# Starting each group's sums with a ScalarE copy into PSUM instead of identity matmuls, and splitting B in place

## The chip, the cores and the metric

The kernel runs on one core of a Trainium2 chip. Its engines work side by side, each through its own queue in order: TensorE (PE) multiplies matrices into the memory called PSUM, VectorE (DVE) does elementwise work and the scans, ScalarE (ACT) does activations and copies, GpSimd (POOL) does elementwise work on SBUF, and SyncE (SP) issues the transfers (DMA). The metric is the device time of one execution in microseconds. Of the kernel before there are three such times, 11,150.11, 11,154.43 and 11,172.63 us; the median is 11,154.43.

## The reference

A hybrid of four layers works on x of shape (4, 64, 64, 96): four images of 64x64 pixels with 96 channels. Layers 0 and 1 are state-space layers, layers 2 and 3 are attention without a softmax followed by a feed-forward network in rounded formats. Each of the first two is x + layer(group_norm(x)), and inside the layer stand an input projection to 192 channels and a gate, a 3x3 depthwise convolution with silu, and then the part that fills the time, a scan over the 4096 pixels in K = 4 orders:

```
x_dbl = einsum('bkdl,kcd->bkcl', xs, x_proj_w)       # xs: the image in the 4 orders
dts, Bs, Cs = split(x_dbl, [R, R + N], axis=2)       # R = 6, N = 16
delta = softplus(einsum('bkrl,kdr->bkdl', dts, dt_w) + dt_b)
def step(h, inp):
    h = exp(dt_t[..., None] * A) * h + (dt_t * u_t)[..., None] * B_t[:, :, None, :]
    y = einsum('bkdn,bkn->bkd', h, C_t)              # sum over the N = 16 states
out_y = ys + Ds.reshape(K, D)[None, :, :, None] * xs # the skip
y = y1 + y2 + y3 + y4                                # the 4 orders, put back in image order
```

In layer 0 the orders are rows, columns and both backwards; in layer 1 they are rows and windows of 2, 4 and 8 pixels. After it come a normalisation over the 192 channels, the gate, and the output projection.

## The kernel before

The scans of layers 0 and 1 run in four phases (`phases`): two layers times two pairs of images. Within a pair, 64 channels of each image fill the 128 partitions, so 192 channels are J = 3 slices j. A phase has 16 blocks (`blocks`): four orders k times four stretches t of TB = 1024 pixels. A block has 48 tiles: for g in 0, 1 (states 0 to 7, then 8 to 15), for j in 0, 1, 2, for the eight states n. That makes 64 blocks and 3072 tiles, and 384 groups of eight tiles.

Each tile works on 128x1024 numbers. ScalarE makes the decays exp(delta*A) (`decays`, line 669). For 11 of the 16 states TensorE spreads a row of B over the partitions into PSUM (`row`, line 662) and VectorE multiplies it by delta*u there (`product`, line 676); for the five states of POOL_N GpSimd multiplies instead (`begin`, line 652). VectorE scans (`scan`, line 684), ScalarE keeps the last state (line 690), GpSimd multiplies the states by C (`weigh`, line 695), and TensorE adds every two tiles into the group's PSUM tile `psY`, of which there is one, with eight matmuls (`gather`, line 727).

The sums of a group do not start from zero. `resume` (line 706) puts into psY what there is so far, by a matmul with the identity: for g = 1 the half sum `ysum` that ScalarE copied out of psY after g = 0 (`flush`, line 739); for g = 0 the sums `yold` of the earlier orders from DRAM, put in this order's pixel order by the operand's view (`resumed` in `pieces`); and for g = 0, k = 0 the convolved image, multiplied by the skip weights through a diagonal matrix `dg` that `skips` makes. After g = 1, `flush` copies the sums back in image order to `ynew` (line 743) and sends them to DRAM. Behind each group's last addition stand thus the flush on ScalarE, then the seed on TensorE, then the next group's first addition.

Once per block `prepare` makes the next block's inputs at fixed tiles: loads, the projection of xs to 76 rows (line 543, PSUM tile `pps`), delta (569 to 582), and a split of B and C into three bfloat16 parts (`parts`) that add up to the float32 value. Part q is cut by ScalarE (`cut`, line 559); `take` (lines 564 and 565) then makes a PSUM tile with the float32 value, by an identity matmul, less the parts so far, by matmuls with `minus`, from which the next part is cut.

The order of every compute engine's queue is written by hand, by a loop over i from -9 to the last tile plus 3. In turn i come begin(i+2), flush(i-3) where a group ends, gather(i-2) for odd tiles, row(i+2), scan(i), the late decays(i+2), product(i+1), weigh(i), the tasks of `prepare` due at this tile, one step of an aside generator (the next phase's convolution, the former phase's normalisation and projection) and last resume(i-2) where a group begins. There are six f tiles, two PSUM tiles `psB`, two `psM` and four `part` tiles (yold, ysum, ynew).

Of the kernel before, what the change touches and what calls it, by code (L numbers as in the profile page):

```python
# [8 lines left out]
F32 = mybir.dt.float32  # L9
# [3 lines left out]
AF = mybir.ActivationFunctionType  # L13
# [21 lines left out]
def kernel(ctx: ExitStack, tc: tile.TileContext, ins, out, layers=(0, 1, 2, 3)):  # L35
    nc = tc.nc
# [7 lines left out]
    def st(shape, dtype, tag, bufs, name=None):  # L44
        return sp.tile(shape, dtype, tag=tag, name=name or tag, bufs=bufs)
# [17 lines left out]
    def part(shape, name):  # L63
        return st(shape, F32, "part", 4, name)
# [44 lines left out]
    minus = wp.tile([96, 2 * N], BF16, tag="minus", name="minus")  # L109
# [25 lines left out]
    W = {}  # L135
# [13 lines left out]

    def skips(li):  # L150

        dsum = small([128, J, 1], "dsum")
        nc.vector.reduce_sum(dsum, W[li]["ds"], axis=mybir.AxisListType.X)
        dg = W[li]["dg"] = st([128, J, 128], F32, "dg", 1)
        for j in range(J):
            nc.scalar.activation(dg[:, j, :], ident, AF.Copy, scale=dsum[:, j, :])

    def tail_weights(li):

# [290 lines left out]
    def pieces(li, k, t):  # L450

        if li == 0:
            if k in (0, 2):
                tt = t if k == 0 else NTB - 1 - t
                img = lambda v: v[:, tt * TB : (tt + 1) * TB]
                view = lambda v: v if k == 0 else v[:, ::-1]
                return img, [(view, lambda o: o)], lambda py, v: [
                    (py[:, s * T : (s + 1) * T], view(v)[:, s * T : (s + 1) * T]) for s in range(2)  # L460
                ]
# [8 lines left out]
            return img, [(view, lambda o: o.rearrange("p (w h) -> p w h", h=HW))], lambda py, v: [  # L470
                (py[:, s * T : (s + 1) * T], view(v)[:, s * cols // 2 : (s + 1) * cols // 2]) for s in range(2)
            ]
        img = lambda v: v[:, t * TB : (t + 1) * TB]
        if k == 0:
            return img, [(lambda v: v, lambda o: o)], None
# [14 lines left out]

        def resumed(py, v):
            v = v.rearrange("p (a i b j) -> p a b i j", i=s, j=s, b=HW // s)
            return [(py[:, a * TB // n : (a + 1) * TB // n], v[:, a]) for a in range(n)]

        return img, [by_row(r) for r in range(s)] if s < n else [by_band(a) for a in range(n)], resumed

    def imaged(li, k, v):

# [2 lines left out]
    def prepare(ph, k, t):  # L501
# [2 lines left out]


        li = phases[ph][0]
        img, views, resumed = pieces(li, k, t)
        p = {"views": views, "img": img, "resumed": resumed, "dus": [None] * J, "deltas": [None] * J}
# [3 lines left out]
        taken = {}  # L512

        def weights():
            if li not in W:
                W[li] = scan_weights(li)
            if t == 0 and k == 0 and "dg" not in W[li]:
# [37 lines left out]
            nc.sync.dma_start(p["bc"][:, halves[s]], rests[s][0 : 4 * N])  # L555

        def cut(s, q):
            of = taken.pop(s) if q else pps[s][0 : 2 * N]
            nc.scalar.copy(p["parts"][32 * q : 32 * q + 32, halves[s]], of)

        def take(s, q):
            of = taken[s] = psM([2 * N, T])
            part = slice(0, 32 * q + 32)
            nc.tensor.matmul(of, ident[0 : 2 * N, 0 : 2 * N], rests[s][0 : 2 * N], start=True, stop=False)
            nc.tensor.matmul(of, minus[part], p["parts"][part, halves[s]], start=False, stop=True)

        def steps(s, j):
            pds.append(psM([128, T]))
# [128 lines left out]

    def recall(i):  # L700
        at, g, j, n = tiles[i]
        ph, k, t = blocks[at]
        sums[at, j] = imaged(phases[ph][0], k, part([128, TB], "yold"))
        nc.sync.dma_start(sums[at, j], made[at]["img"]((yd if k else xcd)[ph][:, j, :]))

    def resume(i):
        at, g, j, n = tiles[i]
        ph, k, t = blocks[at]
        py = sums[at, g, j] = psY()
        old = sums.pop((at, j))  # L710
        of = W[phases[ph][0]]["dg"][:, j, :] if g == 0 and k == 0 else ident
        if g == 0 and k:
            parts = made[at]["resumed"](py, old)
        else:
            parts = [(py[:, s * T : (s + 1) * T], old[:, s * T : (s + 1) * T]) for s in range(2)]
        banks = len(parts) * T // TB
        for m, (o, v) in enumerate(parts):
            nc.tensor.matmul(o, of, v, start=(m % banks == 0), stop=False)  # L718

    def gather(i):  # L720
        at, g, j, n = tiles[i]
        py = sums[at, g, j]
        two = [scanned.pop(e)[1] for e in (i - 1, i)]
        for s in range(2):
            ss = slice(s * T, (s + 1) * T)
            for e in range(2):
                nc.tensor.matmul(  # L727
                    py[64 * e : 64 * e + 64, ss], fold, two[e][:, ss],
                    start=False, stop=(n == g * GN + GN - 1),
                )  # L730

    def flush(i):

        at, g, j, n = tiles[i]
        ph, k, t = blocks[at]
        py = sums.pop((at, g, j))
        if g < NG - 1:
            sums[at, j] = part([128, TB], "ysum")
            nc.scalar.copy(sums[at, j], py)  # L739
            return  # L740
        yb = imaged(phases[ph][0], k, part([128, TB], "ynew"))
        for src, dst in made[at]["views"]:
            nc.scalar.copy(src(yb), dst(py))  # L743
        nc.sync.dma_start(made[at]["img"](yd[ph][:, j, :]), yb)
# [217 lines left out]
    phases = [(li, pair) for li in (0, 1) if li in layers for pair in range(pairs)]  # L962
# [34 lines left out]
    def behind(ph):  # L997
# [9 lines left out]
        if ph + 1 == len(phases):  # L1007
# [4 lines left out]
    tiles = [(at, g, j, n) for at in range(len(blocks)) for g in range(NG) for j in range(J)  # L1012
             for n in range(g * GN, (g + 1) * GN)]
    per = NG * J * GN
    made, reps, sums, states, scanned, order = {}, {}, {}, {}, {}, [None]
    end = len(tiles)
    now, rest = [0], (L - TB) // 256
    with tc.manual_schedule(engines=MANUAL):
        convs = [conv(0)]
        while done[0][0] < TB // T:  # L1020
            next(convs[0])
# [24 lines left out]
        for i in range(-9, end + 4):  # L1046
# [5 lines left out]
                begin(i + 2)  # L1052
            if 0 <= i - 3 < end and tiles[i - 3][3] % GN == GN - 1:
                flush(i - 3)
            if 0 <= i - 2 < end and tiles[i - 2][3] % 2:
                gather(i - 2)
            if 0 <= i + 2 < end:
# [9 lines left out]
            at, place = divmod(i, per)  # L1067
            now[0] = i
            if 0 <= i < end:
# [20 lines left out]
                if aside is not None and not (plan and place in kept):  # L1090
                    advance()
                    if holds == MORE and late_by(i, blocks[at][0]):
                        advance()
            if 0 <= i - 2 < end and tiles[i - 2][3] % GN == 0:
                resume(i - 2)
        now[0] = end + per

        def remaining():
# [113 lines left out]
```

## Time and profile before

| | |
|---|---|
| profiled execution, its own time | 11,149.85 us |
| its span | 11,148.1 us |
| median of three runs | 11,154.43 us |
| mean granted TensorE clock | 0.870 |
| busy PE / DVE / ACT / POOL | 8910.0 / 9926.4 / 6423.1 / 10204.6 us |
| transfers | 66.1% of the 16 DMA engines' time |
| the first scan starts at / the last one | 134.5 us / 10,543.3 us |

A group of instructions is told by its line, engine, operation, written and read tiles, and shapes with its count; then come its busy time in us and the mean of one in ns, then the idle time of its engine just before them and what ended it. In the list of waits the columns are who waited for whom, the sum in us, how many times, and the longest.

### The profile page before, as it was taken

To read this page: it belongs to the slowest core of one execution; us is meant where nothing else is said; L and a number is where in the kernel's file an instruction comes from. 1 tells how busy PE (TensorE), PEld (TensorE's weight loads), DVE (VectorE), ACT (ScalarE), POOL (GpSimd) and SP (SyncE) were. 2 spreads that over 40 slices of the span, in tenths; PEclk is the share of its full clock that TensorE was granted. 3 is DMA by queue.
4 is the path that set the end of the run, shared out by engine and by line. 5 is a ranking of instruction groups with operands and counts; after the bars stand their busy time and mean duration, and the time that the engine had idled before them with its cause. 6 is when DMAs were issued, how large, how long until landed. Compare 5 with 4: busy or idle time off the path is not lost. (4 is left out here: it accounts for less than half of the span.)

```text
span 11148.1 us, 101994 instructions
## 1 busy us (share of the span) xinstructions
PE 8910.0 (80%) x30112; PEld 2880.5 (26%) x30112; DVE 9926.4 (89%) x6431; ACT 6423.1 (58%) x10575; POOL 10204.6 (92%) x5102
## 2 busy tenths in 40 slices
PE   7978888777777779887788878887778877778777
PEld 2222222111222212221222222222222322222365
DVE  3898999999999889989999999999999999999846
ACT  3656556554566646665566656665466655555576
POOL 3989999999999889999999999999999999999846
PEclk8989999888888889998888889998888888888877
DMA  5679976897578885798666656665556565556410
GB/s 134 158 141 162 141 160 157 145 134 136 149 171 151 140 151 149 157 159 132 138 169 157 157 146 169 164 159 143 149 157 156 155 149 148 143 137 159 122 33 22
DMA packets 1848188, 1604.57 MB, mean 144 GB/s; under 512 B 1412298, under 2 KB 1482892, under 8 KB 1847628
## 3 DMA queue, kind: packets, MB, share of 16 engines
q1 hardware_dynamic: 1847628, 1598.04, 66.1%
q8 instruction: 237, 3.88, 0.2%
q14 instruction: 323, 2.65, 0.1%
HBM read 1008.37 MB, written 186.65 MB: 107 GB/s over the span
## 5 line engine op out<-in xcount | busy, mean ns | idle before, releaser
L695 POOL TENSOR_TENSOR f<-f,crep 128x1024 f32<-128x1024 f32 x3072 | 7158.9, 2354 | 395.9 <-DVE f L684 296.6
L727 PE MATMUL psY<-f,fold 128*64 128x512 f32 x12288 | 3795.1, 698 | 183.4 <-POOL f L695 182.8
L684 DVE TENSOR_TENSOR_SCAN f<-f,state,psB 128x1024 f32<-128x1024 f32 x1584 | 3717.8, 2347 | 206.2 <-ACT f L669 50.1
L669 ACT ACTIVATE f<-delta,L_a 128x1024 f32<-128x1024 f32 x2112 | 2406.5, 1145 | 903.9 <-PE psY L727 829.8
L676 DVE TENSOR_TENSOR psB<-psB,du 128x1024 f32<-128x1024 f32 x2112 | 2558.9, 1212 | 362.9 <-PE psB L662 322.1
L662 PE MATMUL psB<-spB,sel 96*128 96x512 bf16 x4224 | 1387.8, 414 | 1613.5 <-DVE f L684 1599.0
L652 POOL TENSOR_TENSOR f<-du,brep 128x1024 f32<-128x1024 f32 x960 | 2265.7, 2360 | 127.2 <-PE psY L727 29.4
L684 DVE TENSOR_TENSOR_SCAN f<-psB,state,f 128x1024 f32<-128x1024 f32 x720 | 1676.7, 2329 | 76.8 <-POOL f L652 50.3
L727 PEld LDWEIGHTS psY<-f,fold 128*64 128x64 f32 x12288 | 974.9, 154 | 2525.3 <-issue 1806.8
L690 ACT COPY state<-f 128x1 f32<-128x1 f32 x2304 | 429.7, 188 | 2065.8 <-DVE f L684 2056.7
L669 ACT ACTIVATE psB<-delta,L_a 128x1024 f32<-128x1024 f32 x960 | 1070.2, 1115 | 696.0 <-DVE f L684 636.1
L684 DVE TENSOR_TENSOR_SCAN f<-f,psB 128x1024 f32<-128x1024 f32 x528 | 1208.3, 2288 | 57.6 <-ACT f L669 5.9
L662 PEld LDWEIGHTS <-sel 96*128 96x128 bf16 x4224 | 271.3, 99 | 3320.4 <-DVE f L684 2163.7
L289 PE MATMUL psM<-pad,wf 96*64 96x512 f32 x3456 | 901.4, 623 | 36.0 <-ACT pad L283 28.9
L684 DVE TENSOR_TENSOR_SCAN f<-psB,f 128x1024 f32<-128x1024 f32 x240 | 545.6, 2273 | 102.9 <-ACT psB L669 60.0
L718 PE MATMUL psY<-ysum,ident 128*128 128x512 f32 x768 | 554.5, 862 | 98.3 <-ACT ynew L743 86.7
L585 POOL TENSOR_TENSOR xs<-delta,xs 128x1024 f32<-128x1024 f32 x192 | 452.7, 2358 | 95.0 <-ACT delta L582 95.0
L569 PE MATMUL psM<-proj,dtw 12*128 12x512 f32 x768 | 455.2, 686 | 0.0
L543 PE MATMUL psM<-xs,xp 128*76 128x512 f32 x768 | 414.7, 651 | 5.5 <-DMA xs<-xcd 4.2
L718 PE MATMUL psY<-yold,ident 128*128 128x512 f32 (+2 forms) x960 | 370.6, 526 | 42.2 <-ACT ysum L739 26.7
L289 PEld LDWEIGHTS psM<-pad,wf 96*64 96x64 f32 x3456 | 221.4, 138 | 501.0 <-issue 422.6
L743 ACT COPY ynew<-psY 128x1024 f32<-128x1024 f32 (+2 forms) x312 | 242.4, 818 | 171.5 <-PE psY L727 171.5
(149 smaller groups left out, 6644.6 us busy)
## 6 DMA issues: line engine op xcount, KB each, us to landing
crep<-bc SPq DMA_DIRECT2D x2048, 256.0 KB, 4.8
delta<-delta SPq DMA_DIRECT2D x768, 256.0 KB, 4.8
du<-xs SPq DMA_DIRECT2D x768, 256.0 KB, 6.2
brep<-bc SPq DMA_DIRECT2D x640, 256.0 KB, 4.9
yd<-ynew SPq DMA_DIRECT2D x192, 512.0 KB, 7.8
xraw<-xcd SPq DMA_DIRECT2D x144, 512.0 KB, 8.5
yold<-yd SPq DMA_DIRECT2D x144, 512.0 KB, 8.9
xcd<-xo SPq DMA_DIRECT2D x96, 256.0 KB, 3.0
```

The source lines that it names most:

```text
L289: nc.tensor.matmul(px[64 * i : 64 * i + 64], w["wf"][:, tap, 64 * j : 64 * j + 64], pads[i][0][:, tap // 3 : tap // 3 + rows, tap % 3 : ta ...
L569: nc.tensor.matmul(pds[-1], order[0][1][64:76, j, :], rests[s][64:76], start=True, stop=True)
L585: nc.gpsimd.tensor_mul(xs[j], deltas[j], xs[j])
L652: nc.gpsimd.tensor_mul(f[:, 1:], made[at]["dus"][j][n % 2], reps[at, 0, n])
L662: nc.tensor.matmul(scanned[i][0][:, ss], sel[:, n, :], made[at]["parts"][:, ss], start=True, stop=True)
L669: nc.scalar.activation(out, made[at]["deltas"][j][n % 2], AF.Exp, scale=W[phases[ph][0]]["a"][:, k, j, n // 2 : n // 2 + 1])
L676: nc.vector.tensor_mul(scanned[i][0], scanned[i][0], made[at]["dus"][j][n % 2])
L684: nc.vector.tensor_tensor_scan(f[:, 1:], a, bu, 0.0 if t == 0 else states[at - 1][:, c : c + 1], ALU.mult, ALU.add)
L690: nc.scalar.copy(states[at][:, c : c + 1], f[:, TB : TB + 1])
L695: nc.gpsimd.tensor_mul(f[:, 0:TB], f[:, 1:], reps[at, 1, n])
L718: nc.tensor.matmul(o, of, v, start=(m % banks == 0), stop=False)
L727: nc.tensor.matmul(py[64 * e : 64 * e + 64, ss], fold, two[e][:, ss], start=False, stop=(n == g * GN + GN - 1),)
```

## The change

The seed of a group's sums moves from TensorE to ScalarE: `resume` now copies the sums so far into psY with ScalarE, scaled by the skip weight itself where k = 0, in the views of `pieces` for the other orders. `dg` and `resumed` go. Since no matmul starts psY's accumulation any more, `unlock` writes all of psY with matmuls once at the very start, and `gather` adds to what is there. In the loop `resume(i-2)` moves from the end of the turn to just behind the flush of the group before. Beside it, `take` no longer makes a PSUM tile of its own: it subtracts each part from the projection's own PSUM tile, where `cut` reads the next one.

```diff
     def skips(li):
-        dsum = small([128, J, 1], "dsum")
+        dsum = W[li]["skip"] = small([128, J, 1], "dsum")
         nc.vector.reduce_sum(dsum, W[li]["ds"], axis=mybir.AxisListType.X)
-        dg = W[li]["dg"] = st([128, J, 128], F32, "dg", 1)
-        for j in range(J):
-            nc.scalar.activation(dg[:, j, :], ident, AF.Copy, scale=dsum[:, j, :])
...
         def cut(s, q):
-            of = taken.pop(s) if q else pps[s][0 : 2 * N]
-            nc.scalar.copy(p["parts"][32 * q : 32 * q + 32, halves[s]], of)
+            nc.scalar.copy(p["parts"][32 * q : 32 * q + 32, halves[s]], pps[s][0 : 2 * N])
 
         def take(s, q):
-            of = taken[s] = psM([2 * N, T])
-            part = slice(0, 32 * q + 32)
-            nc.tensor.matmul(of, ident[0 : 2 * N, 0 : 2 * N], rests[s][0 : 2 * N], start=True, stop=False)
-            nc.tensor.matmul(of, minus[part], p["parts"][part, halves[s]], start=False, stop=True)
+            part = slice(32 * q, 32 * q + 32)
+            nc.tensor.matmul(
+                pps[s][0 : 2 * N], minus[part], p["parts"][part, halves[s]], start=False, stop=True,
+                skip_group_check=True,
+            )
...
+    def unlock():
+        py = psY()
+        for s in range(2):
+            for q in range(T // 128):
+                o = s * T + q * 128
+                nc.tensor.matmul(py[:, o : o + 128], ident, ident, start=(q == 0), stop=True, skip_group_check=True)
+
...
         py = sums[at, g, j] = psY()
         old = sums.pop((at, j))
-        of = W[phases[ph][0]]["dg"][:, j, :] if g == 0 and k == 0 else ident
-        if g == 0 and k:
-            parts = made[at]["resumed"](py, old)
+        if g:
+            nc.scalar.copy(py, old)
+        elif k == 0:
+            nc.scalar.activation(py, old, AF.Copy, scale=W[phases[ph][0]]["skip"][:, j, :])
         else:
-            parts = [(py[:, s * T : (s + 1) * T], old[:, s * T : (s + 1) * T]) for s in range(2)]
-        banks = len(parts) * T // TB
-        for m, (o, v) in enumerate(parts):
-            nc.tensor.matmul(o, of, v, start=(m % banks == 0), stop=False)
+            for src, dst in made[at]["views"]:
+                nc.scalar.copy(dst(py), src(old))
...
                     py[64 * e : 64 * e + 64, ss], fold, two[e][:, ss],
-                    start=False, stop=(n == g * GN + GN - 1),
+                    start=False, stop=(n == g * GN + GN - 1), skip_group_check=True,
...
     with tc.manual_schedule(engines=MANUAL):
+        unlock()
         convs = [conv(0)]
...
                 flush(i - 3)
+            if 0 <= i - 3 < end and tiles[i - 3][3] % GN == GN - 1 and i - 2 < end or i == 2:
+                resume(i - 2)
             if 0 <= i - 2 < end and tiles[i - 2][3] % 2:
                 gather(i - 2)
...
-            if 0 <= i - 2 < end and tiles[i - 2][3] % GN == 0:
-                resume(i - 2)
```

More of the change, by code (lines that the diff above doesn't have):

```diff
@@ L458, in pieces @@
                 view = lambda v: v if k == 0 else v[:, ::-1]
-                return img, [(view, lambda o: o)], lambda py, v: [
-                    (py[:, s * T : (s + 1) * T], view(v)[:, s * T : (s + 1) * T]) for s in range(2)
-                ]
+                return img, [(view, lambda o: o)]
             cols = TB // HW
@@ L468, in view @@
                 return v if k == 1 else v[:, ::-1, ::-1]
-            return img, [(view, lambda o: o.rearrange("p (w h) -> p w h", h=HW))], lambda py, v: [
-                (py[:, s * T : (s + 1) * T], view(v)[:, s * cols // 2 : (s + 1) * cols // 2]) for s in range(2)
-            ]
+            return img, [(view, lambda o: o.rearrange("p (w h) -> p w h", h=HW))]
         img = lambda v: v[:, t * TB : (t + 1) * TB]
         if k == 0:
-            return img, [(lambda v: v, lambda o: o)], None
+            return img, [(lambda v: v, lambda o: o)]
         s = 1 << k
@@ L489, in by_band @@
             )
[L491 to L495, printed above, removed]
+        return img, [by_row(r) for r in range(s)] if s < n else [by_band(a) for a in range(n)]
     def imaged(li, k, v):
@@ L506, in prepare @@
         li = phases[ph][0]
-        img, views, resumed = pieces(li, k, t)
-        p = {"views": views, "img": img, "resumed": resumed, "dus": [None] * J, "deltas": [None] * J}
+        img, views = pieces(li, k, t)
+        p = {"views": views, "img": img, "dus": [None] * J, "deltas": [None] * J}
         xs, deltas = [], []
@@ L511, in prepare @@
         raws, pps, rests, pds = [], [], [], []
-        taken = {}
         def weights():
@@ L516, in weights @@
                 W[li] = scan_weights(li)
-            if t == 0 and k == 0 and "dg" not in W[li]:
+            if t == 0 and k == 0 and "skip" not in W[li]:
                 skips(li)
```

## The prediction, made before the result was known

> **What bounds the kernel now.** I read the page's busy times first, then engines by stretch, then the list of waits, then the groups by form of the lines that the diff touches, and last the timeline around one place where a group of eight states ends.
>
> ```profile
> PE 8910.0 (80%) x30112; PEld 2880.5 (26%) x30112; DVE 9926.4 (89%) x6431; ACT 6423.1 (58%) x10575; POOL 10204.6 (92%) x5102
> ...
> 135.00:351.00 216.00, 184.13 (x672) 53.51 (x672) 146.86 (x94) 104.41 (x153) 152.38 (x66) 0.92 0.55 139
> 1522.00:1676.00 154.00, 132.87 (x438) 35.53 (x438) 146.69 (x87) 95.25 (x140) 152.81 (x67) 0.93 0.74 170
> 5430.00:5599.00 169.00, 125.63 (x392) 39.53 (x392) 148.46 (x87) 96.85 (x185) 155.43 (x71) 0.87 0.65 154
> 9439.00:9901.00 462.00, 343.99 (x990) 97.99 (x990) 445.78 (x244) 240.57 (x373) 458.00 (x199) 0.85 0.59 146
> ```
>
> The columns of a stretch are its length, then busy PE, PEld, DVE, ACT, POOL, then granted clock. 154 us is one block (48 tiles) that runs well: POOL is busy for 152.8 of it. Three such blocks in a row (9439 to 9901) have POOL busy for 458 of 462. So a block has a floor of about 154 us, set by POOL, and nothing that PE or ACT saves can be seen there. What can be won lies in blocks above the floor: the first one (216 us, PE busy 184 beside the convolution) and those beside the normalisation and output projection (169 us and the like). Between 700 and 10400 us POOL is idle for 457 us (9700 less 9243 busy), in the first two blocks for 83 more (216+173 less 152.4+153.3). These 540 us are all that can be had from the scan.
>
> ```profile
> ACT f L669 <- PE psY L727: 829.8, 479, 6.0
> DVE psB L676 <- PE psB L662: 322.1, 242, 13.6
> POOL f L695 <- DVE f L684: 296.6, 212, 26.1
> DVE f L684 <- ACT psB L669: 84.2, 26, 26.1
> DVE f L684 <- ACT f L669: 57.9, 31, 8.0
> ```
>
> VectorE waits for TensorE's spread of B (L662) for 322 us, and GpSimd for VectorE's scan for 297. VectorE waits for ScalarE for only 142.
>
> ```profile
> 5006.51 3.68 PE L718 MATMUL psY<-yold,ident 128*128 128x512 f32 x4
> ...
> 5010.12 1.94 PE L727 MATMUL psY<-f,fold 128*64 128x512 f32 x8
> ...
> 5011.99 0.61 PE L662 MATMUL psB<-spB,sel 96*128 96x512 bf16 x2
> ...
> 5012.17 1.15 ACT L669 ACTIVATE f<-delta,L_a 128x1024 f32<-128x1024 f32 x1 [2.20 <-PE psY L727]
> ...
> 5012.63 1.23 DVE L676 TENSOR_TENSOR psB<-psB,du 128x1024 f32<-128x1024 f32 x1 [1.25 <-PE psB L662]
> ```
>
> Here the seed of the sums (L718), the first pair's addition (L727) and the next spread of B (L662) follow each other on PE without a gap; then ACT has waited 2.20 us for an f buffer and VectorE 1.25 us for its product. Numbering the scans in time and giving each wait of L676 to the scan after it, tile 5 of the eight (the first spread behind the seed in PE's queue) takes 111 us of VectorE's wait for PE and tile 6 takes 58: 169 us in 132 waits, the rest spread over six other places.
>
> **The change part by part.**
>
> ```profile
> L718 PE MATMUL psY<-ysum,ident 128*128 128x512 f32 x768 | 554.5, 862 | 98.3 <-ACT ynew L743 86.7 <-ACT state L690 10.0 <-ACT ysum L739 1.7
> L564 PE MATMUL psM<-proj,ident 32*32 32x512 f32 x512 | 273.2, 614 | 0.0
> L739 ACT COPY ysum<-psY 128x1024 f32<-128x1024 f32 x192 | 193.1, 1006 | 135.5 <-PE psY L727 121.0 <-issue 12.3 <-DMA brep<-bc 1.2
> L669 ACT ACTIVATE psB<-delta,L_a 128x1024 f32<-128x1024 f32 x960 | 1070.2, 1115 | 696.0 <-DVE f L684 636.1 <-PE psY L727 38.2 <-issue 11.0
> L743 ACT COPY ynew<-psY 128x1024 f32<-128x1024 f32 x120 | 163.2, 1360 | 101.3 <-PE psY L727 101.3
> ```
>
> *Seed leaves PE.* The five forms of L718 are busy 554.5+273.0+103.3+49.7+47.9 = 1028 us, 2.68 us at each of 384 boundaries. In the trace the first addition begins right behind the last seed matmul at all of them, on average 3.6 us after ScalarE's flush has ended.
>
> *Seed arrives on ACT.* No row shows a plain copy from SBUF into PSUM. Nearest are the plain copy out of PSUM (1.006 us) and the exponential into PSUM (1.115). So: 192 copies for g=1 at 1.006 = 193; 48 scaled ones (k=0) at 1.115 = 54; layer 0: 24 reversed at 1.01 = 24 and 48 transposed at 1.9 (the L743 row is 72 at 1.0 and 48 of these: 163.2-72 = 91) = 91; layer 1 in pieces: 96 of 512 elements at 0.58 = 56 and 96 of 256 at 0.378 = 36. Together 454 us, 1.18 per boundary; ACT goes from 6423 to some 6880 us (62%). With 1.115 for the plain ones it would be 475.
>
> *Where it stands in ACT's queue.* The seed now follows the flush at once; behind it are the state copy, decays into psB, and work of the asides. In 265 of 384 flushes the next ACT instruction follows within 0.3 us, so it is pushed by all 1.18. I pushed each by its seed's time, let ACT's later idle time absorb it, and set it against the time that each decay stands ready before its scan (median 2.2 us at the tightest places): VectorE would be late in 39 boundaries, 28 us in all. Taken: 28. Bounds: 0 (PE's earlier additions also end ACT's 830 us of waiting for f, so ACT may run earlier than before), and 1.18 at each of the 265, 313 us.
>
> *Seed to first addition.* The addition now waits for flush plus 1.18 us instead of 3.6: 2.4 us earlier, and so are the next spread of B and the release of f. If two thirds of the 169 us at tiles 5 and 6 go, VectorE is given 113 us. One third may stay because PE, arriving earlier, waits for ACT or GpSimd instead. Bounds: 0, and all 309 us of L676's waits in the scan.
>
> *What VectorE's time is worth.* From the third block on POOL is idle for 487 us and DVE for 715 (every gap over 0.03 us, initial two blocks left out): 0.68. So 113 gives 77, and the 28 cost 19. Bounds 0 and 1.
>
> *Split of B in place.* 512 ident matmuls (273 us) go; the 256 of L565 stay (64x32 and 32x32 weights take the same, 398 and 384 ns). They can run before the cut that L565 waits for, so they lie under ACT's work, save where PE is full. Same with the psM buffer that each took. The projection keeps both psM buffers until its last cut, in places where no aside runs; the steps behind it took them at the same places before. I count nothing but PE time; bounds -34 us (what ACT's L559 waits for L565 now) to +34.
>
> *First two blocks.* There PE is busy 184 of 216 and 158 of 173. It loses 16+4 us per block (1028 and 273 over 64). Half of it on the path: -20; bounds 0 and -40.
>
> *The rest.* Three 0.39 us scalings of ident per layer go: nothing. Eight unlocking matmuls of 0.3 us (the 128x128 form of L360) stand before the first convolution, whose inputs are then still being loaded: nothing, at most 2.4 us. No DMA is added or moved; yold has 31 us (nine tiles) from its issue to its use and lands in 8.5, so SP and POOL queues stay as they are.
>
> **A rule that speaks against it.** A less busy PE gets a lower clock in this trace: 0.93 at 86% busy (1522 to 1676) and 0.85 at 74% (9439 to 9901). PE at (8910-1301)/11150 = 68% would by that line fall from 0.87 to about 0.81, and 7609 us of matmuls become some 8170. PE keeps 740 us of its 1301, and I have the third that stays above for this. The Trainium skill (TensorE: Matmul & The Clock Gate, Part 1) has it that one idle window of about 3.4 us halves the clock. By that rule a boundary that goes idle would run its additions at half speed (1.94 us for eight becoming 3.37, as once at 5021 us); met at half of the boundaries, 1.43 of the 2.4 us would go there, and the 77 would be an estimated 54; by the rows it stays 77. The skill's PSUM page (summary of rules) advises against seeds that ScalarE writes, since its writes do not set the accumulate bits. No run here shows it, and the unlocking matmuls are there for that; either way no time changes.
>
> **Sum.** 11,149.9 (profiled execution; 0.04% under the median 11,154.4) -77 -20 +19 = 11,072 us. Against the 540 us that could be had this is a sixth.
>
> **The rivals.** *Much more is won:* earlier additions end most L676 waits and f waits. All 309 x 0.68 = 210, first blocks 40: 10,900. For it: the waits named; against: much of POOL's idle time is beside DMA and group statistics, which stay. *Nothing to be seen:* POOL hides it, 11,150 +-22. For it: the blocks at 154; against: those at 169. *Slower:* ScalarE's queue becomes what is late at each boundary. At its price, 313 x 0.68 = 213 against 97 won: 11,266. It decides from 0.37 us of VectorE's time per boundary on (97/0.68/384). For it: 265 flushes with ACT work close behind; against: median slack 2.2 us. *It does not do what it says:* with accumulate flags wrong the sums are wrong, the time the same.
>
> **How the numbers follow.** 0.2% (22 us) is about what a measurement of this kernel tells from no change. Likeliest case (11,000 to 11,128) 0.50; much more won 0.15; nothing 0.17; slower 0.18. The range takes half of each outer case: 10,960 to 11,190; the likeliest alone is 11,000 to 11,128. Faster 0.65, same 0.17, slower 0.18.
>
> **What would show it.** L718 gone from PE, PE near 8200 us, clock near 0.81, ACT near 6880; waits of L676 for L662 from 322 to about 200; waits of L684 for ACT from 142 to some 170; POOL's idle time 80 us less; blocks at 154 us unmoved, the first one some 10 us shorter. Wrong if waits for L669 pass 300 us, or if PE's first addition waits for ACT at most boundaries and L676's waits stay.

## The result and the profile after

The kernel with the change takes 11,231.25 us (median of four runs, 11,218.49 to 11,249.81) and the one before, run beside it, 11,163.53. The ratio is 1.0062 with an interval of 1.0039 to 1.0085: slower by 0.6%, where 11,072 us and a range up to 11,190 had been forecast. The profiled execution took 11,219.25 us (span 11,216.4) at a mean granted clock of 0.817.

The functions keep their names and get other lines: the scan is now L671, the product L663, the spread of B L649, the additions L722, the weighing L682, the decays L656, the matmuls to delta L556 with their ScalarE reader L563, the split's subtraction L549, and the seed L708 to L713. Below are the busy times of the page after:

```profile
PE 8392.2 (75%) x27696; PEld 2658.5 (24%) x27696; DVE 9925.7 (88%) x6431; ACT 6880.5 (61%) x11073; POOL 10199.9 (91%) x5102
```

VectorE and GpSimd do the work they did before (9926.4 and 10204.6 us), so the 68 us more are idle time of theirs. ScalarE has grown to the 6880 us that were forecast. TensorE lost 1301 us of matmuls and its busy time fell by only 518. The groups by form show where these stand (count, then busy us and mean ns of one, then idle time before them). Before, the additions and the matmuls to delta read:

```profile
L727 PE MATMUL psY<-f,fold 128*64 128x512 f32 x12288 | 3795.1, 698 | 183.4 <-POOL f L695 182.8
...
L569 PE MATMUL psM<-proj,dtw 12*128 12x512 f32 x768 | 455.2, 686 | 0.0
```

and after:

```profile
L722 PE MATMUL psY<-f,fold 128*64 128x512 f32 x12288 | 4271.3, 771 | 588.7 <-POOL f L682 264.9 <-issue 242.7 <-POOL f L639 43.2
...
L556 PE MATMUL psM<-proj,dtw 12*128 12x512 f32 x768 | 533.9, 793 | 0.2 <-ACT spB L545 0.2
...
L708 ACT COPY psY<-ysum 128x1024 f32<-128x1024 f32 x192 | 195.2, 1017 | 6.1
L713 ACT COPY psY<-yold 128x1024 f32<-128x1024 f32 x72 | 116.0, 1611 | 2.3
...
L710 ACT ACTIVATE psY<-yold,dsum 128x1024 f32<-128x1024 f32 x48 | 53.7, 1118 | 1.5
```

Together with two smaller forms of L713 (56.6 and 36.1 us) the seeds take 457.6 us of ScalarE; 454 had been worked out. The additions are the same 12,288 matmuls as before and take 771 ns each in place of 698; the matmuls to delta take 793 in place of 686. What stayed on TensorE thus grew from 7609 to 8392 us. Of the waits (who waited for whom, sum in us, times and longest) this is one before:

```profile
ACT delta L576 <- PE psM L569: 45.9, 57, 2.0
```

and after they read:

```profile
DVE psB L663 <- PE psB L649: 307.1, 220, 12.3
POOL f L682 <- DVE f L671: 301.9, 199, 27.7
...
ACT delta L563 <- PE psM L556: 143.2, 133, 2.8
DVE f L671 <- ACT psB L656: 140.2, 52, 27.8
...
DVE f L671 <- ACT f L656: 78.6, 38, 6.9
```

VectorE's wait for the spread of B, 322.1 us before, was to fall to about 200 and fell by 15. The wait for delta, 45.9 before, has trebled (143.2), though nothing was added in front of those matmuls. VectorE's waits for ScalarE rose from 142 to 219, still below the 300 that would have spoken for ScalarE's queue.

**Where the time goes, place by place.** I numbered the scans in time and took, for every place p in a block (counted from 0 to 47), the time between scan p and the next, after less before, summed over blocks 2 to 62; "tile 24" in such a sum is the step from scan 24 to scan 25, in which VectorE waits for tile 25's spread. The sum is +64.6 us. Tiles 4 and 5 of each eight, the boundary tiles, whose steps contain the waits behind the seed and the first addition in TensorE's queue, win 107.9 us. Everything else taken together loses 172.5: tiles 22 to 27 lose 51.4 (tile 24 alone 0.58 us per block, 35 in all), tiles 8 to 11 lose 40.8, 30 and 31 lose 23.4, 16 to 19 lose 19.8, 38 and 39 lose 18.4, the rest 18.7. In front of those blocks, the first scan starts at 128.4 in place of 134.5 us, block 0 takes 223.9 in place of 216.3 and block 1 171.2 in place of 173.3.

So the gain at the boundaries came, and more than that was lost elsewhere. This is TensorE's timeline around tile 24 of block 58, before (start, length, what it is, and in brackets the idle time ahead of it and what ended it):

```profile
9661.85 1.04 PE L564 MATMUL psM<-proj,ident 32*32 32x512 f32 x2
9662.82 0.39 PE L565 MATMUL psM<-spB,minus 64*32 64x512 bf16 x1
9664.39 0.60 PE L662 MATMUL psB<-spB,sel 96*128 96x512 bf16 x2 [1.19 <-DVE f L684]
9664.93 1.12 PE L569 MATMUL psM<-proj,dtw 12*128 12x512 f32 x2
9665.98 1.94 PE L727 MATMUL psY<-f,fold 128*64 128x512 f32 x8
9667.85 0.61 PE L662 MATMUL psB<-spB,sel 96*128 96x512 bf16 x2
```

and the same place after:

```profile
9714.30 0.39 PE L549 MATMUL psM<-spB,minus 32*32 32x512 bf16 x1
9718.51 0.82 PE L649 MATMUL psB<-spB,sel 96*128 96x512 bf16 x2 [3.83 <-DVE f L671]
9719.26 2.07 PE L556 MATMUL psM<-proj,dtw 12*128 12x512 f32 x2
9721.26 3.68 PE L722 MATMUL psY<-f,fold 128*64 128x512 f32 x8
9724.87 0.94 PE L649 MATMUL psB<-spB,sel 96*128 96x512 bf16 x2
```

and VectorE's next product after:

```profile
9725.85 1.23 DVE L663 TENSOR_TENSOR psB<-psB,du 128x1024 f32<-128x1024 f32 x1 [1.58 <-PE psB L649]
```

Without the identity matmuls of the split, TensorE idles 3.83 us here, where it had idled 1.19. The two matmuls to delta then take 2.07 us in place of 1.12, and the eight additions 3.68 in place of 1.94. The spread for the next tile, which comes behind them in TensorE's queue, is so late that VectorE stands still for 1.58 us. There are holes of more than 2.5 us ahead of tile 24's spread in none of the 61 blocks before and in 31 after; in all places, from the third block to the last scan, they grew from 221 to 337. Between the scans of tiles 24 and 26 the mean granted clock fell from 0.859 to 0.778.

### The profile page after: what moved, and what is told of

The parts are those of the page before. It is cut to its first block, busy times and chain, and to the rows that moved or that the text cites. A ratio compares the mean times of both kernels' runs of the same rounds, so it can differ in the third digit from the quotient of the medians.

```text
span 11216.4 us, 97704 instructions
## 1 busy us (share of the span) xinstructions
PE 8392.2 (75%) x27696; PEld 2658.5 (24%) x27696; DVE 9925.7 (88%) x6431; ACT 6880.5 (61%) x11073; POOL 10199.9 (91%) x5102
## 3 DMA queue, kind: packets, MB, share of 16 engines
q8 instruction: 218, 3.57, 0.1%
## 5 line engine op out<-in xcount | busy, mean ns | idle before, releaser
L682 POOL TENSOR_TENSOR f<-f,crep 128x1024 f32<-128x1024 f32 x3072 | 7156.5, 2354 | 428.7 <-DVE f L671 301.9
L722 PE MATMUL psY<-f,fold 128*64 128x512 f32 x12288 | 4271.3, 771 | 588.7 <-POOL f L682 264.9
L671 DVE TENSOR_TENSOR_SCAN f<-f,state,psB 128x1024 f32<-128x1024 f32 x1584 | 3717.7, 2347 | 216.2 <-ACT f L656 62.5
L649 PE MATMUL psB<-spB,sel 96*128 96x512 bf16 x4224 | 1478.2, 438 | 1912.4 <-DVE f L671 1877.6
L663 DVE TENSOR_TENSOR psB<-psB,du 128x1024 f32<-128x1024 f32 x2112 | 2557.7, 1211 | 345.1 <-PE psB L649 307.1
L656 ACT ACTIVATE f<-delta,L_a 128x1024 f32<-128x1024 f32 x2112 | 2405.7, 1144 | 660.5 <-PE psY L722 582.9
L722 PEld LDWEIGHTS psY<-f,fold 128*64 128x64 f32 x12288 | 1099.3, 167 | 3049.6 <-issue 2141.4
L671 DVE TENSOR_TENSOR_SCAN f<-psB,state,f 128x1024 f32<-128x1024 f32 x720 | 1677.5, 2330 | 121.8 <-ACT psB L656 60.9
L656 ACT ACTIVATE psB<-delta,L_a 128x1024 f32<-128x1024 f32 x960 | 1068.7, 1113 | 630.5 <-DVE f L671 588.7
L671 DVE TENSOR_TENSOR_SCAN f<-f,psB 128x1024 f32<-128x1024 f32 x528 | 1208.5, 2289 | 66.6 <-ACT f L656 13.0
L649 PEld LDWEIGHTS <-sel 96*128 96x128 bf16 x4224 | 282.8, 101 | 3773.9 <-DVE f L671 2513.8
L286 PE MATMUL psM<-pad,wf 96*64 96x512 f32 x3456 | 928.4, 639 | 60.9 <-ACT pad L280 45.7
L671 DVE TENSOR_TENSOR_SCAN f<-psB,f 128x1024 f32<-128x1024 f32 x240 | 545.4, 2273 | 118.7 <-ACT psB L656 76.1
L556 PE MATMUL psM<-proj,dtw 12*128 12x512 f32 x768 | 533.9, 793 | 0.2 <-ACT spB L545 0.2
L563 ACT ACTIVATE delta<-psM,L_dtb 128x512 f32<-128x512 f32 x384 | 261.3, 681 | 144.0 <-PE psM L556 143.2
L734 ACT COPY ysum<-psY 128x1024 f32<-128x1024 f32 x192 | 193.1, 1006 | 144.4 <-PE psY L722 130.0
```

Of the source, the lines that this page charges most:

```text
L286: nc.tensor.matmul(px[64 * i : 64 * i + 64], w["wf"][:, tap, 64 * j : 64 * j + 64], pads[i][0][:, tap // 3 : tap // 3 + rows, tap % 3 : ta ...
L556: nc.tensor.matmul(pds[-1], order[0][1][64:76, j, :], rests[s][64:76], start=True, stop=True)
L649: nc.tensor.matmul(scanned[i][0][:, ss], sel[:, n, :], made[at]["parts"][:, ss], start=True, stop=True)
L656: nc.scalar.activation(out, made[at]["deltas"][j][n % 2], AF.Exp, scale=W[phases[ph][0]]["a"][:, k, j, n // 2 : n // 2 + 1])
L663: nc.vector.tensor_mul(scanned[i][0], scanned[i][0], made[at]["dus"][j][n % 2])
L671: nc.vector.tensor_tensor_scan(f[:, 1:], a, bu, 0.0 if t == 0 else states[at - 1][:, c : c + 1], ALU.mult, ALU.add)
```

## The experiments

The theory (the clock): TensorE with less to do stands idle longer ahead of the stretch where it is needed most, is granted a lower clock there, and its own matmuls then come late for VectorE. The rivals: ScalarE's copies delay its queue; the split or the seed does harm by its order alone (a wait for a PSUM tile, a matmul moved); or there is nothing but an even slowing in proportion to the clock's mean.

### The seed alone, and the split alone

The kernel after with the old split, and the kernel before with the split in place. The diff is that of the first against the kernel after; that of the second against the kernel before is the same the other way round.

```diff
+        taken = {}
...
         def take(s, q):
-            part = slice(32 * q, 32 * q + 32)
-            nc.tensor.matmul(
-                pps[s][0 : 2 * N], minus[part], p["parts"][part, halves[s]], start=False, stop=True,
...
+            of = taken[s] = psM([2 * N, T])
+            part = slice(0, 32 * q + 32)
+            nc.tensor.matmul(of, ident[0 : 2 * N, 0 : 2 * N], rests[s][0 : 2 * N], start=True, stop=False)
+            nc.tensor.matmul(of, minus[part], p["parts"][part, halves[s]], start=False, stop=True)
```

> The changed kernel with the split of B as before (the identity matmul and a PSUM tile of its own). Clock theory (the matmuls taken away leave TensorE idle at fixed tiles, its granted clock falls, and what queues next runs slow; the split opens the worst such hole, at tiles 22 and 23 of a block): 11,110 to 11,170 us, granted clock about 0.83, VectorE's wait for the spread of B at tile 25 back from 62 to about 30 us. ScalarE theory (the copies into PSUM make ScalarE late at each boundary): at least 11,215 us, and VectorE's waits for ScalarE stay at some 219 us.

> The kernel before with the split of B in place, and nothing else of the change. Clock theory: 30 to 70 us slower than before (11,195 to 11,235 us) with the clock down from 0.87 to about 0.85 and the wait at tile 25 up from 29 to some 60 us. ScalarE theory: no slower than before (11,130 to 11,165 us).

The seed alone takes 11,207.4 us, 1.0038 times the kernel before (1.0024 to 1.0052), and the split alone 11,219.4, 1.0055 times (1.0043 to 1.0067). Both halves lose. The split, which had been priced at nothing, loses 0.0055 x 11,150 = 61 us (48 to 75) although it takes away 273 us of work and adds none. For the seed alone the clock theory had expected a gain or none (11,110 to 11,170), and that was missed. By places, the split alone loses 61.1 us at tiles 22 to 27 (tile 24: 0.68 us per block), and what it wins and loses elsewhere adds up to +0.8; the seed alone wins 107.6 at the boundaries and loses 38.9 at tiles 22 to 27 and 52.6 at 8 to 11. The loss at tile 24 is as large with the seed alone (0.56 us per block) as with the whole change (0.58), although the split's identity matmuls stand in their old place there: either half is enough for it, and the two do not add up. These are two waits of the split alone (its product is L675, its spread L661):

```profile
DVE psB L675 <- PE psB L661: 383.0, 291, 13.3
...
ACT delta L575 <- PE psM L568: 121.9, 109, 2.8
```

VectorE's wait for the spread of B is 383 us against 322 before: the 61 us. The wait for delta is 121.9, against 45.9 before.

### ScalarE's copies alone

The kernel before, its TensorE seed kept, with two ScalarE copies, each of half the same old sums, at the place where the seed stands after. They go to a bfloat16 scratch tile that nobody reads, so ScalarE has the load and nobody waits for it.

```diff
+    spoil = wp.tile([128, T], BF16, tag="spoil", name="spoil")
+
+    def extra(i):
...
+            nc.scalar.copy(out, half)
...
+            if 0 <= i - 3 < end and tiles[i - 3][3] % GN == GN - 1 and i - 2 < end:
+                extra(i - 2)
```

> The kernel before, its seed by matmuls kept, with two ScalarE copies of half the old sums each (into a scratch tile that nobody reads) where the changed kernel has its seed: ScalarE's added load alone, 384 times about 1.2 us. ScalarE theory: 65 us slower or more (11,225 us up), with VectorE's waits for ScalarE up from 142 to about 220 us. Clock theory: at most 25 us slower, clock 0.87 as before.

It takes 11,170.5 us: 1.0004 (0.9995 to 1.0014). Its groups and two waits:

```profile
L730 ACT CAST spoil<-ysum 128x512 bf16<-128x512 f32 x384 | 238.7, 622 | 6.1
...
L730 ACT CAST spoil<-yold 128x512 bf16<-128x512 f32 x382 | 237.5, 622 | 6.0
```

```profile
DVE f L684 <- ACT psB L669: 117.1, 38, 26.1
...
DVE f L684 <- ACT f L669: 64.6, 34, 8.0
```

ScalarE does 476 us more, where the seeds take 458, and VectorE waits 182 us for it in place of 142. That is 40 us of waits and 0.04% of time, where this rival had asked for 65 us or more: the rival of ScalarE's queue falls.

### No seed at all

The kernel before with `resume` only taking psY and dropping the old sums, and the first addition of a group starting from zero.

```diff
-        ph, k, t = blocks[at]
-        py = sums[at, g, j] = psY()
-        old = sums.pop((at, j))
...
-            nc.tensor.matmul(o, of, v, start=(m % banks == 0), stop=False)
+        sums[at, g, j] = psY()
+        sums.pop((at, j))
...
-                    start=False, stop=(n == g * GN + GN - 1),
+                    start=(n == g * GN + 1), stop=(n == g * GN + GN - 1),
```

> The kernel before without any seed: the sums of a group start from zero, so the earlier orders, the half sums and the skips are left out of the result. No identity matmuls and no ScalarE copies for it; the split of B as before. Clock theory (what TensorE loses is enough to slow it): no faster than before, 11,165 to 11,215 us, near the kernel with the seed alone (11,207), clock about 0.83. Chain theory (the first addition now waits for ScalarE's copy, and that costs): faster than before, 11,060 to 11,140 us.

Taking 1028 us off TensorE and putting nothing in its place gives 11,207.1 us, 1.0038 (1.0025 to 1.0051), the same as the seed alone with all its copies (11,207.4). Its page and additions:

```profile
PE 8604.0 (77%) x28192; PEld 2693.3 (24%) x28192; DVE 9920.0 (88%) x6431; ACT 6430.0 (57%) x10575; POOL 10201.4 (91%) x5102
```

```profile
L718 PE MATMUL psY<-f,fold 128*64 128x512 f32 x12288 | 4247.6, 768 | 363.1 <-POOL f L695 197.0 <-ACT state L690 63.5 <-ACT ynew L734 57.2
```

Only TensorE's work has gone, no engine has more to do, and the kernel is slower. The additions are as slow as after (768 ns). VectorE's waits for ScalarE are 207 us here too, without one copy: most of what had looked in the profile after like the copies' price comes without them.

### Giving the split its TensorE time back

The kernel after with a float32 matmul with zero weights, as large as the identity matmul that went, ahead of each subtraction.

```diff
+    nought = wp.tile([64, 2 * N], F32, tag="nought", name="nought")
+    nc.vector.memset(nought, 0.0)
...
             nc.tensor.matmul(
+                pps[s][0 : 2 * N], nought[part], rests[s][part], start=False, stop=False,
+                skip_group_check=True,
+            )
+            nc.tensor.matmul(
```

> The changed kernel with a float32 matmul of the size of the removed identity one put back ahead of each subtraction of the split, with zero weights (it adds nothing): TensorE's work of the split returns, its PSUM tiles do not. Clock theory: half or more of the loss goes, 11,150 to 11,200 us, clock about 0.83. ScalarE theory: as the changed kernel, 11,220 to 11,245 us. If it is the PSUM tiles of the split that cost, also 11,220 to 11,245 us, but with the kernel of the seed alone fast.

11,190.9 us, 1.0036 (1.0022 to 1.0049): the median falls by 0.26% for useless work added to the kernel after, to about what the seed alone takes. The two intervals overlap a little (1.0039 to 1.0085 without it), so the time alone says little. At tiles 22 to 27 the loss falls from 51.4 to 20.4 us, with the order of the split and its PSUM tile as in the kernel after. That speaks for the time that TensorE no longer spends there; for the 20 us that remain it shows nothing.

### Filling all the holes

Six bfloat16 matmuls with zero weights into psY, which leave its sums as they are, behind the last addition and ahead of the spread for tiles 2, 8, 16, 18, 24, 30, 37 and 46, where many of the holes over 2.5 us stand (tile 37, one of GpSimd's, has no spread). They went into the kernel after, the one before, and the one with the split's TensorE time given back (the last of the three expectations).

```diff
+    WARM, COUNT = (2, 8, 16, 18, 24, 30, 37, 46), 6
...
+    def warm(i):
+        at, g, j, n = tiles[i]
+        py = sums[at, g, j]
+        for m in range(COUNT):
+            ss = slice(m % 2 * T, (m % 2 + 1) * T)
+            nc.tensor.matmul(py[:, ss], nought, sel[:, 0:4, :], start=False, stop=False, skip_group_check=True)
...
+            if 0 <= i - 2 < end and i + 2 < end and (i + 2) % per in WARM:
+                warm(i - 2)
             if 0 <= i + 2 < end:
                 row(i + 2)
```

> The changed kernel with six bfloat16 matmuls of zero weights, which add nothing to the sums, ahead of the spread of B at eight tiles of a block (2, 8, 16, 18, 24, 30, 37, 46), where TensorE of the changed kernel sits idle for more than 2.5 us. Clock theory: 40 us or more faster than the changed kernel (11,140 to 11,190 us), clock 0.84 to 0.87, fewer slow additions and steps. Chain theory: as the changed kernel or slower, 11,225 to 11,270 us.

> The kernel before with the same matmuls of zero weights at the same eight tiles. Clock theory: a little faster than before, 11,110 to 11,155 us, clock near 0.90. If the clock is not what counts: as before or slower, 11,165 to 11,210 us.

> The changed kernel with both fillings: zero-weight float32 matmuls ahead of each subtraction of the split, and the zero-weight bfloat16 ones at eight tiles. Clock theory: faster than the changed kernel with only the first (11,191 us), 11,090 to 11,160 us, so that the seed's gain at the boundaries shows. Chain theory: no faster than 11,190 us.

The kernel after: 11,188.3 us, 1.0017 (1.0005 to 1.0029). The one before: 11,245.5, 1.0077 (1.0065 to 1.0089), where the clock theory had expected 11,110 to 11,155. The third: 11,197.0, 1.0035 (1.0020 to 1.0050), where 11,090 to 11,160 had been expected. The filling wins 0.45% on the kernel after and costs the one before 0.77%, so a higher mean clock is not worth anything by itself: before went from 0.870 to 0.889 and became slower. By places the filled kernel before wins 37.2 us at tiles 22 to 27 and loses 131.8 at the boundaries, 1.59 us per block at tile 29 alone, behind the filling for tile 30: there TensorE had stood idle for only 0.25 us on average, and the filling made its queue longer. The filled kernel after wins 49 at tiles 22 to 27 against the kernel after and gives back 75 of its 108 at the boundaries (by an execution of 11,218.9 us, 31 over its median). The even-slowing theory falls with this, and the places have to be taken one by one.

### Filling one hole

The same lines with a count for each tile, `WARM = {24: 14}`, on the kernel after; with six matmuls at tile 24 alone on the kernel before; with eight on the seed alone; and with 6 at tiles 2, 8 and 16 beside the 14 at 24 on the kernel after (after_warm4).

> The changed kernel with fourteen zero-weight bfloat16 matmuls (about 3 us) in one place of a block only, ahead of the spread of B for tile 24, where the changed kernel's TensorE sits idle for some 3.8 us before the steps to delta. Clock theory: the 0.58 us per block that tile 24 lost, and part of the 0.26 at tile 26, come back: 30 to 60 us faster than the changed kernel (11,170 to 11,200 us); steps that run at half speed fall from 33% to 15% or less. If TensorE's clock is not the cause: the changed kernel's 11,231 us or more.

> The kernel before with six zero-weight matmuls at tile 24 only (the filling at eight tiles won 0.53 us per block there, and lost 1.59 at tile 29, where its matmuls for tile 30 stood in a full queue). Clock theory: 15 to 40 us faster than before, 11,125 to 11,150 us. Otherwise 11,160 to 11,185 us.

> The kernel with the seed alone on ScalarE (split as before) and eight zero-weight matmuls at tile 24. Clock theory: 25 to 50 us faster than without them (11,207 us), 11,155 to 11,180 us. Otherwise 11,200 us up.

> The changed kernel with zero-weight matmuls ahead of tiles 2, 8 and 16 (six each) and 24 (fourteen), leaving out the places where they only lengthened TensorE's queue (18, 30, 37, 46). Clock theory: 50 to 90 us faster than the changed kernel (11,140 to 11,180 us), clock near 0.85. If the idle places at 2, 8 and 16 cost nothing: as with tile 24 alone.

| kernel | median us | ratio to before, interval | tiles 22-27 | boundary tiles | all blocks 2-62 |
|---|---|---|---|---|---|
| after | 11,231.3 | 1.0062 (1.0039 to 1.0085) | +51.4 | -107.9 | +64.6 |
| split alone | 11,219.4 | 1.0055 (1.0043 to 1.0067) | +61.1 | -12.0 | +61.9 |
| seed alone | 11,207.4 | 1.0038 (1.0024 to 1.0052) | +38.9 | -107.6 | +54.6 |
| after, 14 at tile 24 | 11,115.4 | 0.9961 (0.9947 to 0.9974) | -33.6 | -117.4 | -59.5 |
| after, 2, 8, 16 and 24 | 11,119.9 | 0.9964 (0.9952 to 0.9977) | -31.5 | -119.4 | -41.5 |
| seed alone, 8 at tile 24 | 11,139.5 | 0.9987 (0.9978 to 0.9996) | +0.4 | -118.8 | -25.1 |
| before, 6 at tile 24 | 11,158.1 | 0.9998 (0.9989 to 1.0006) | -34.7 | +31.7 | +5.8 |

The last three columns are sums of differences to the kernel before, in us, from one profiled execution each, worked out as above. These executions lie up to 14 us from their kernels' medians (the kernel after 12 under, the seed alone 9 over, "after, 14 at tile 24" 14 under). 14 useless matmuls at one place per block turn the kernel after from 0.6% slower into 0.4% faster, and it beats both kernels. The expectations were missed on the good side for the three kernels with the seed on ScalarE (11,170 to 11,200, 11,140 to 11,180 and 11,155 to 11,180 us for 11,115, 11,120 and 11,139) and on the other for the kernel before (11,125 to 11,150 for 11,158). This is TensorE's timeline of the kernel after with 14 matmuls at tile 24, at the same place of block 58:

```profile
9608.33 0.38 PE L551 MATMUL psM<-spB,minus 32*32 32x512 bf16 x1
9608.64 3.20 PE L736 MATMUL psY<-sel,nought 96*128 96x512 bf16 x14
9611.67 0.60 PE L651 MATMUL psB<-spB,sel 96*128 96x512 bf16 x2
9612.21 1.12 PE L558 MATMUL psM<-proj,dtw 12*128 12x512 f32 x2
9613.26 2.07 PE L724 MATMUL psY<-f,fold 128*64 128x512 f32 x8
9615.26 0.61 PE L651 MATMUL psB<-spB,sel 96*128 96x512 bf16 x2
```

The 3.20 us of zeros lie where the hole was; the matmuls to delta are back at 1.12 us, and the additions take 2.07 in place of 3.68. Between the scans of tiles 24 and 26 the granted clock is 0.980, and three of its waits, with the scan's line now L673, are:

```profile
POOL f L684 <- DVE f L673: 255.7, 162, 27.7
...
DVE psB L665 <- PE psB L651: 210.0, 156, 10.9
...
ACT delta L565 <- PE psM L558: 60.6, 72, 3.0
```

VectorE's wait for the spread of B is now close to the 200 that the prediction had wanted from the change itself, in part because 28.5 us of waits at tile 24 are gone that the kernel before has too. The kernel before, with six matmuls there, wins as much against itself at tiles 22 to 27 (34.7), and loses it again at the boundaries (31.7), where its seed still stands on TensorE. Its time is the same as without. So the filling is no gain in itself on that kernel; on the kernel after it lets the change's own gain through. With the hole filled, the kernel with the split in place stands at 0.9961 and the one without at 0.9987, whereas unfilled they stand at 1.0062 and 1.0038; but one has 14 matmuls there and the other 8, and the 8 lengthen the step at tile 23 by 25 us in all, so this does not show what the split is worth. Filling ahead of tiles 2, 8 and 16 as well wins nothing further; why not, no run tells.

**Block by block.** In the profile's records the clock is either full or half. Counting a block as one at half clock where its mean between the spreads of tiles 24 and 25 is under 0.75, the traces give, over blocks 2 to 62:

| kernel | blocks at half clock | step at tile 24 in these / in the others, us | longest idle time of TensorE ahead of tile 24's spread, us |
|---|---|---|---|
| before | 37 | 4.44 / 3.56 | 1.97 |
| after | 51 | 4.90 / 3.55 | 4.43 |
| split alone | 51 | 5.01 / 3.55 | 4.07 |
| seed alone | 51 | 4.87 / 3.58 | 2.22 |
| no seed | 48 | 4.98 / 3.59 | 2.12 |
| after, 14 at tile 24 | 7 | 3.69 / 3.57 | 1.29 |

So the step is long where the clock is at half, in the kernel before too (the seven blocks of the last row are the exception), and one long hole is not needed for that: the seed alone has none over 2.22 us there. What the clock records follow is how busy TensorE is over a window. They change only at multiples of 3.41 us; while the scans run, every window at full clock in which TensorE was busy for less than 40% was followed by one at half (251 of 251 before, 353 of 353 after), and of those in which it was busy for at least half, 145 of 1942 and 111 of 1451.

## Why the prediction was wrong

**The mechanism at the boundary was right.** The five forms left TensorE, ScalarE got 457.6 us for the 454 forecast, and the tiles behind the seed won 107.9 us, against 77 forecast. VectorE's wait for the spread of B fell there by 113 us (154.7 to 41.9 in blocks 2 to 62), as forecast, though the "two thirds" had been a guess; nearly all of it came off those steps, where the factor of 0.68 had let 77 through.

**ScalarE's queue was priced somewhat too high in the span.** I had taken 28 us of VectorE's time, 19 in the span. The copies alone brought 40 us of waits and 0.04% (-0.05 to 0.14). The rival that ended nearest to the result (11,266 us, by ScalarE's queue) therefore has the wrong mechanism.

**The step that failed is the price of the lower clock.** It stands in the sum at two places. For the split of B it was nothing: "I count nothing but PE time; bounds -34 us (what ACT's L559 waits for L565 now) to +34." Measured alone the split costs 61 us (48 to 75). I looked for who waits for those identity matmuls and found nobody, and did not ask what they did for the matmuls behind them: without them a hole of 3.8 us stands just ahead of a dense stretch. For the seed it was only the third of 169 us that was to stay at the boundaries, and nothing anywhere else. That is the larger miss: measured alone the seed's move costs 42 us (27 to 58) where the sum had a gain, because it loses 162 us outside the boundaries against the 108 that it wins there; 38.9 of them are lost at tiles 22 to 27.

**The paragraph on the clock had the size and not the place.** Forecast were 0.81 and a PE near 8200 us; measured were 0.817 and 8392 (what stays grew by 10% in place of 7). But I set the lost time against the 1301 us removed, as a sum over the whole kernel, and concluded that "PE keeps 740 us of its 1301". That sum means nothing where TensorE has time to spare, and hides what happens at tile 24, where it has none. The share of additions over 0.9 us went from 0.195 to 0.347, and of matmuls to delta over 0.9 us from 0.107 to 0.327. The Trainium skill (TensorE: Matmul & The Clock Gate, Part 1), by which an idle window of about 3.4 us halves the clock, fits the place shown above: behind the 3.83 us hole matmuls take 1.8 to 1.9 times as long (2.07 against 1.12, 3.68 against 1.94), behind the 1.19 us one they do not. But the window need not be idle: in these traces one busy for less than 40% was enough each time, and the seed alone slows tile 24 without a hole over 2.22 us. I had weighed the rule at the boundaries, where the change was made, and got 54 in place of 77; the boundaries won 108, and the clock told at other places.

**VectorE's wait for the spread of B, 322 to about 200: wrong as the change stands (307).** With the hole filled it is 210, though not by the boundaries alone. The wait that went at the boundaries was replaced by waits at other tiles: at tiles 22 to 27 it grew from 35.8 to 84.7 us, at 30 and 31 it grew by about 20, at 38 and 39 from 13.2 to 30.8. GpSimd's idle time from the third block on, forecast 80 us less, is 67 more (486 to 553).

**First two blocks, -20: wrong.** Block 0 is 7.7 us longer, block 1 2.1 shorter. I took TensorE at 184 of 216 us for the bound there. It is busy 178 of the same stretch after, at a clock of 0.88 for 0.92, and VectorE's busy time there falls too, from 147 to 143, as the block stretches beyond it:

```profile
135.00:351.00 216.00, 178.22 (x638) 51.35 (x637) 142.77 (x91) 109.33 (x156) 147.54 (x65) 0.88 0.50 131
```

**What the sum makes of it.** Blocks 2 to 62: -107.9 at the boundaries, +51.4 at tiles 22 to 27 and +121.1 elsewhere = +64.6; the start -6.1, blocks 0 and 1 +5.6, block 63 -1.2, so that the last scan starts 62.9 us later (10,606.2 for 10,543.3); behind it +5.5: 68.4 us, where the spans differ by 68.3.

**What is settled and what is open.** Shown: ScalarE's copies cost nothing that can be measured; taking TensorE's work away costs time with nothing in its place; the loss at tiles 22 to 27 goes with the clock; and filling the hole ahead of tile 24 wins 1.0% on the kernel after (0.9961 against 1.0062, each to the kernel before beside it) and nothing on the one before. Of the 172.5 us lost outside the boundaries these tiles are 51.4. Likely, though no run changed it there alone: the 41.8 us at tiles 30, 31, 38 and 39 go the same way. Counted as at tile 24, the blocks at half clock rise from 0 to 51 at tile 30 (its step 4.16 us in these, 3.62 in the others) and from 14 to 36 at tile 38 (4.43 and 3.74). Open: the 41 us at tiles 8 to 11, where VectorE's waits for ScalarE's decays grow from 16 to 49 us and are 55 without any seed, so that the copies are not needed for them. They come with the seed's leaving (51.6 without any seed, 2.2 with the split alone), stand in few blocks (block 27 alone 10.7), and stay at 34 with the hole ahead of tile 8 filled. The 20 us at tiles 16 to 19 and the 19 in the rest were not settled either, nor why the kernel before loses at tile 29 when only tile 24 is filled (0.39 us per block). They may be the price of waits that move on to another engine; no run tells.

## What to carry to other kernels

Work on an engine that does not set the pace can still be what keeps it quick: before removing it, look in that engine's timeline for the idle time that it leaves (over some microseconds together, not in single holes alone), for what stands dense behind that, and for who waits for the last of it. A mean clock and a busy share say little here; compare the two traces place by place within the repeated block, since gains and losses of 100 us can hide in a sum of 60. And where idle time ahead of a dense stretch is the suspicion, a few matmuls with zero weights in that one hole are both the test and, sometimes, the cure; put where the engine has hardly any idle time they cost time (0.77% on the kernel before).

## What the runs showed of the hardware

- Taking 1028 us of matmuls off a TensorE that is busy for 80% of the span, with nothing in their place, made the kernel 0.38% slower; taking 273 us off it made it 0.55% slower.
- Matmuls with zero weights count as work for the granted clock: 14 of them in 3.20 us brought it from 0.778 to 0.980 between the scans of tiles 24 and 26.
- The granted clock is full or half and changes at multiples of 3.41 us. Of the windows at full clock with TensorE busy for less than 40%, all were followed by half (251 before, 353 after); of the windows at half in which it was busy for less than 70%, none led back to full (146 and 210).
- ScalarE's plain copy of 128x1024 float32 into PSUM takes 1017 ns, about as long as the one out of it (1006); the 72 whose source is read reversed or transposed take 1611 ns on average.
